# Turning the rows of 36 steps by DMA, over two 16-bit planes, in place of TensorE; and a first weight block loaded in quarters

## The chip, the cores and the metric

The kernel runs on one core of a Trainium2 chip. The metric is the time of one execution on the device in microseconds (us), less being better. The time before is 2451.24 us, the median of three runs (2449.57 to 2452.58).

## The reference

Input x has 128 sequences of 64 steps with 512 values each. Two layers are added to it in turn. Cut to what matters:

```python
# layer 0: a GRU over the 64 steps, then a linear layer with ternary weights
hs = gru(cond, x, W_ih, W_hh, b_ih, b_hh)           # 64 steps, one after another
x = x + einsum('bsi,oi->bso', hs, ternary(weight)) + bias
# layer 1: a causal convolution over the steps, then a mixture of experts
c = depthwise_causal_conv(x, cond) + b               # [128, 64, 512]
scores = softmax(c @ gate_w.T)                       # 64 experts, the best 6 per row
routed = sum over chosen experts of score * (silu(r @ w_gate) * (r @ w_up)) @ w_down   # at most 64 rows each
shared = silu(c @ sw_gate) * (c @ sw_up) @ sw_down   # 512 -> 704 -> 512, for all 8192 rows
x = x + routed + shared
```

## The kernel before

The work goes through one core in stages. First come the 64 steps of the GRU (loop over t, up to about 1220 us of the span), with the weights split into planes of fewer bits. Then comes the convolution (`conv_group`, to about 1280 us), as products with small Toeplitz matrices; it leaves its result c in SBUF, in two tiles `hids` of 32 steps each. `hid(t)` is the slice of step t: 128 sequences on the partitions, 512 values of 4 bytes along the row.

From there on the kernel goes through the 64 steps in 16 groups of NB = 4 (`shared(i)`, i from 0 to 15). Each group computes the shared expert with Winograd's seven products in place of eight (`winograd`, called by `Block.product` for up and gate and by `Down.product` for the way back). A product is two f32 matmuls of 256 columns; `PIECES` (44) is about the number of pieces that one `shared(i)` yields. Products add up in few PSUM buffers (`psx`, `psw`, `psz`, `y`), and VectorE and ScalarE take them out in between: `u2` (L853), `u3` (L858), `g1` (L864), `g2` (L867), `two` (L870). TensorE can't start the next sum in a buffer before that.

A product needs the values along the partitions, so the rows of each step are turned first. That is what `turn(t)` does, with four TensorE transposes of 128x128 into PSUM (L1128), and `route` copies them back over `hid(t)` on VectorE (L1138). From step TH = 32 on the turned rows also go to `xts` in HBM (L1144), for the second half of the groups. `route(its)` then computes the router's `lg` products (L1152), the softmax and the six best experts, for the groups `its`; `tab<-sc` stores the scores (L1196). `routing()` calls it for groups 2i+1 and 2i+2 while `shared(i)` runs (i from 0 to 7), and the main loop takes one step of it at every 44/20 of a piece. The memory of a group that is done is free for others: `sums_space(i)` uses the rows of group i-2 for the sums of the Winograd products, and `add_shared(i)` adds a group's result to the output with a DMA from GpSimd's queue (L1106).

What runs when is set by a planner: the instructions are recorded in the order of the program, and it then puts them in order on each engine by expected times and by priorities (`tc.issue_after` binds some). Each engine, and each engine's queue of DMA issues, then keeps to that order.

At the start the kernel loads the first step's input `xp` and the weights of the input gates, `raw_i[0]`, `raw_i[2]`, `raw_i[1]`, in halves of 512 KB (`load_halves`), all on SP's queue. TensorE's first products (`psy`) need `xp` and `raw_i[0]`, and VectorE and ScalarE split the weights into planes (`convert`).

Of the kernel before, what the change touches and what calls it, by code (L numbers as in the profile page):

```python
# [9 lines left out]
BF16 = mybir.dt.bfloat16  # L10
I32 = mybir.dt.int32
U8 = mybir.dt.uint8
F32R = mybir.dt.float32r
AF = mybir.ActivationFunctionType
ALU = mybir.AluOpType
# [4 lines left out]
P = 128  # L20
B = 128
T = 64
D = 512
KD = D // P
# [23 lines left out]
def adaln_ffn_kernel(  # L48
# [22 lines left out]
    nc = tc.nc  # L71
# [10 lines left out]
    xts = dram.tile([T // 2, P, D], F32, name="xts")  # L82
# [10 lines left out]
        out=before,  # L93
        in_=before,
# [11 lines left out]
    def load_rows(dst, src):  # L106

        return nc.sync.dma_start(out=dst, in_=src.rearrange("(k p) n -> p k n", p=P))
# [98 lines left out]
    HK = KD // 2  # L207
    HD = D // 2
    gis_ = ExitStack()
    ps_gi = gis_.enter_context(tc.tile_pool(name="ps_gi", bufs=1, space=PSUM))  # L210
    with (
# [19 lines left out]
        def planes(pool, name):  # L231
            return [pool.tile([P, KD, D], F32R, name=f"{name}{n}") for n in "hls"]

# [7 lines left out]
        raw_i = [st.tile([P, KD, D], F32, name=f"rawi{c}") for c in range(3)]  # L241
# [9 lines left out]
        cols = [slice(c * D, (c + 1) * D) for c in range(3)]  # L251
        xps, xns, parts_of = {}, {}, {}

        def load_xt(t, queue=nc.gpsimd):
            xps[t] = xpp.tile([P, KD, B], F32, name="xp")
            queue.dma_start(out=xps[t], in_=xT[t])
# [34 lines left out]
        def repeated(dst, row):  # L291
            nc.sync.dma_start(out=dst, in_=row.partition_broadcast(P))

        def load_halves(dst, src):
            for k in range(2):
                load_rows(dst[:, k * HK : (k + 1) * HK], src[k * HD : (k + 1) * HD])

        h = el0.tile([P, D], F32, name="h")
        bh = {0: io0.tile([P, D], F32, name="xn"), 1: el0.tile([P, D], F32, name="n")}

        load_xt(0, nc.sync)
        load_halves(raw_i[0], w_ih[:, cols[0]])
        load_halves(raw_i[2], w_ih[:, cols[2]])
        nc.sync.dma_start(out=h, in_=cond)
        load_xt(1, nc.sync)
        load_halves(raw_i[1], w_ih[:, cols[1]])
        load_rows(raw_h[0], w_hh[:, cols[0]])
        repeated(br, b_ih[cols[0]])
        repeated(bh[0], b_hh[cols[0]])
# [20 lines left out]
        def banks(c):  # L330
            pool = ps_gh if c == 1 else ps_gi
            return [pool.tile([P, D], F32, name=n) for n in BANKS[c]]
# [37 lines left out]
        def split_x(t):  # L370

            xp = xps.pop(t)
            cut = xpp.tile([P, KD, B], F32, name="xcut", bufs=1)
            parts_of[t] = [el0.tile([P, KD, B], F32R, name=f"x{n}") for n in "hls"]
            xh, xl, xs = parts_of[t]
# [46 lines left out]
        def place(t, n):  # L422

            if t < T - TAIL:
                return xpp.tile([P, KD, B], F32R, name=f"h{n}", bufs=1)
            return el0.tile([P, KD, B], F32R, name=f"x{n}")

# [63 lines left out]
        def cell_n(t, ps, r):  # L491
            a, b = ps
            n = el0.tile([P, D], F32, name="n")
            if a is None:
                nc.vector.tensor_add(n, b, bhn)
            else:
                nc.vector.scalar_tensor_tensor(n, a, WHOLE, bhn, ALU.mult, ALU.add)
                nc.vector.tensor_add(n, b, n)
            nc.vector.tensor_mul(n, n, r)
            nc.vector.tensor_add(n, n, gis.pop((t, 2)))  # L500
            nc.scalar.activation(n, n, AF.Tanh)  # L501
            nc.vector.tensor_sub(h, h, n)
            return n
# [15 lines left out]
        for c in (0, 2, 1):  # L519
            a, b = banks(c)  # L520
# [15 lines left out]
        n = cell_n(0, (None, first[2][1]), r)  # L536
# [41 lines left out]
        for t in range(1, T):  # L578
# [18 lines left out]
            n = cell_n(t, ps_n, r)  # L597
# [11 lines left out]
            if t in (1, 2):  # L609
# [9 lines left out]
                else:  # L619
                    sgn = wh0.enter_context(  # L620
                        tc.tile_pool(name="sgn", bufs=1, reuse_waits="tile")
                    ).tile([P, KD, D], F32R, name="sgn")
                    wf = wi.tile([P, KD, D], F32, name="q")
# [37 lines left out]
    TH = T // 2  # L661


    cum = ctx.enter_context(tc.tile_pool(name="cum", bufs=1)).tile([P, T, NE], U8, name="cum")
    first = ExitStack()
# [9 lines left out]
    def hid(t):  # L675
        return hids[t // TH][:, t % TH, :]
# [21 lines left out]
    with tc.tile_pool(name="ps_c", bufs=4, space=PSUM) as ps_c:  # L698
        for sl in range(NSL):
# [6 lines left out]
            for g in range(DS // 4):  # L706
# [4 lines left out]
                d = slice(g * 4, g * 4 + 4)  # L711
# [9 lines left out]
            if sl >= TAIL_AT:  # L721
# [3 lines left out]
                d = slice(0 if sl == TAIL_AT else 2 * DS * sl, 2 * DS * (sl + 1))  # L725
# [3 lines left out]
            for n in range(2):  # L729
                if sl == NSL - 2 + n:  # L730
                    d = slice(2 * DS * sl, 2 * DS * (sl + 1))
# [61 lines left out]
    NB = 4  # L793
# [3 lines left out]
    def behind(instructions, when=True):  # L797
        return tc.issue_after(instructions[-1].ins) if when and instructions else nullcontext()
# [303 lines left out]
    PIECES = 7 * full + 9  # L1102

    def add_shared(i):
        for t in range(i * NB, i * NB + NB):
            nc.gpsimd.dma_start(out=out_t[t], in_=rows_of(i)[:, t % NB], accum_op=ALU.add)  # L1106


    with (
# [10 lines left out]
        def turn(t):  # L1120

            if t in (2, 3):
                ps = ps_y.tile([P, D], F32, name="y")
            else:
                ps = ps_t1.tile([P, D], F32, name="pst1")
            ps = ps.rearrange("p (k b) -> p k b", k=KD)
            for k in range(KD):
                last = nc.tensor.transpose(ps[:, k, :], hid(t)[:, k * P : (k + 1) * P], ident)  # L1128
            return ps, last

        def route(its, turned={}):


            for i in its:
                for t in range(i * NB, i * NB + NB):
                    ps = turned[t] if t in turned else turn(t)[0]
                    with behind(marks, t in turned):
                        copied = nc.vector.tensor_copy(  # L1138
                            hid(t).rearrange("p (k b) -> p k b", k=KD), ps
                        )  # L1140
                    if t == NB - 1:
                        marks.append(copied)
                    if t >= TH:
                        nc.sync.dma_start(out=xts[t - TH], in_=hid(t))  # L1144
                    yield
# [21 lines left out]
            for n, i in enumerate(its):  # L1167
# [27 lines left out]
                for a in range(2):  # L1195
                    nc.sync.dma_start(  # L1196
                        out=tab_t[i * NB + 2 * a : i * NB + 2 * a + 2, :, D:].rearrange(
                            "t b e -> b t e"
                        ),
                        in_=sc[:, a::2, :NE],  # L1200
# [7 lines left out]
                for j in range(NB):  # L1208
                    t, r = i * NB + j, 2 * (j % 2) + j // 2
# [17 lines left out]
        def put_rows(i):  # L1227
            if i < NI:

                with tc.issue_after(loaded.ins):  # L1230
                    for t in range(i * NB, i * NB + NB):
                        (nc.gpsimd if i == 1 else nc.sync).dma_start(
                            out=tab_t[t, :, :D], in_=hid(t)
                        )
# [5 lines left out]
        for j in range(2):  # L1240
            nc.sync.dma_start(out=swdr[j * rest : (j + 1) * rest, :], in_=sw_down[full * P :, :])

        ahead = route([0])
        for _ in range(NB):
            next(ahead)
# [8 lines left out]
        for i in range(NI // 2):  # L1254
            put_rows(2 * i + 3)
            put_rows(2 * i + 4)

            def routing():
                if i == 0:
                    yield from ahead  # L1260
                its = [r for r in (2 * i + 1, 2 * i + 2) if r < NI]
                yield from route(its, second if i == 0 else {})

            routing_ = routing()
            done = 0
            for n, _ in enumerate(shared(i)):
                if done * PIECES <= n * 20:
                    with behind(products or marks, i == 0):
                        next(routing_, None)
                    done += 1  # L1270
            for _ in routing_:
                pass
            add_shared(i)
# [325 lines left out]
    for i in range(NI // 2 + 1, NI):  # L1599
        n = i - NI // 2 - 1  # L1600
        sums = None
        if i == NI - 1:
# [3 lines left out]
                out=sums, in_=out_t[i * NB : (i + 1) * NB].rearrange("t b d -> b t d")  # L1606
# [58 lines left out]
```

## Time and profile before

| | before |
|---|---|
| median of 3 runs | 2451.24 us (2449.57 to 2452.58) |
| profiled execution, its own time | 2452.42 us |
| its span | 2450.7 us |
| granted TensorE clock, mean | 0.999 |
| instructions | 32124 |
| TensorE transposes `pst<-ident,hid` and `y<-ident,hid` (L1128) | 256 |
| VectorE copies back (L1138) | 64, of 0.69 us |

The profile is one execution, so its times are compared with its own time and not with the median. PE is TensorE, PEld its weight loads (which overlap PE), DVE VectorE, ACT ScalarE, POOL GpSimd, SP the engine that issues most DMAs. In a line of a group, "out<-in" are the program's names, then come shapes and count, the busy time in us and the mean of one in ns, then the idle time before these instructions and what ended it. A line of the timeline has start, duration, engine, line, operation and count; one of the chain has start, duration and what. In a line of windows the numbers after an engine are busy us and, in brackets, instructions.

### The profile page before, as it was taken

How to read it: one execution, taken by the hardware profiler on the slowest of the kernel's cores; microseconds unless marked ns; L12 is line 12 of the kernel's file. 1: busy time of each engine (PE TensorE's matmuls, PEld its weight loads, DVE VectorE, ACT ScalarE, POOL GpSimd, SP SyncE). 2: the span in 40 equal slices, each digit the busy share in tenths (PEclk: the TensorE clock that was granted, in tenths of full speed). 3: DMA queues.
4: the chain of work that ended last, by engine and by line, in shares of the span. 5: the costliest groups of instructions: out<-in, count | busy, mean ns of one | idle time of the engine just before them, and what ended most of it. 6: DMA issues, size and time to landing. Idle time of an engine off the chain costs nothing.

```text
span 2450.7 us, 32124 instructions
## 1 busy us (share of the span) xinstructions
PE 2436.9 (99%) x12317; PEld 1883.7 (77%) x12317; DVE 1546.5 (63%) x3073; ACT 463.1 (19%) x847; POOL 445.8 (18%) x468
## 2 busy tenths in 40 slices
PE   9999999999999999999999999999999999999999
PEld 5888888888888888888896688888876666666667
DVE  8877777777777776777686566666653433343344
ACT  5211111111111111111122222222211111111111
POOL 1122221122112112211220000000012222222220
PEclk9999999999999999999999999999999999999999
DMA  5244443333232223222497112222468999899962
GB/s 183 68 95 81 82 80 63 61 69 65 56 61 56 56 56 62 56 52 52 142 343 270 24 23 44 62 59 61 116 174 287 300 290 312 267 330 293 283 175 52
DMA packets 464456, 322.33 MB, mean 132 GB/s; under 512 B 316592, under 2 KB 384176, under 8 KB 462128
## 3 DMA queue, kind: packets, MB, share of 16 engines
q1 hardware_dynamic: 435408, 246.34, 35.6%
q0 software_dynamic: 28896, 73.95, 13.5%
q8 instruction: 97, 1.59, 0.3%
q14 instruction: 55, 0.45, 0.1%
HBM read 233.44 MB, written 92.03 MB: 133 GB/s over the span
## 4 chain that ended last, share of the span: by engine, by line
PE 98%; DMA 1%; DVE 0%; issue 0%; ACT 0%; SPq 0%; POOL 0%; DVEq 0%; ACTq 0%
PE psa L336 9%; PE psx L336 9%; PE psw L336 9%; PE psx L824 8%; PE psw L824 8%; PE psz L824 8%; PE psy L336 5%; PE psb L336 5%; PE psz L336 5%; PE psf L336 5%; PE y L824 4%; PE py L1550 3%; PE pg L1524 3%; PE pu L1524 3%; PE y L1001 2%; PE psc L193 2%
## 5 line engine op out<-in xcount | busy, mean ns | idle before, releaser
L1534 DVE SCALAR_TENSOR_TENSOR a<-a,rw,pu 128x352 f32<-128x352 f32 x32 | 18.6, 580 | 213.4 <-PE pu L1524 213.4
L354 DVE SCALAR_TENSOR_TENSOR xs<-xl,xcut 128x512 fp32r<-128x512 f32 x63 | 103.6, 1644 | 66.0 <-POOL xl L353 66.0
L347 DVE TENSOR_SCALAR hcut<-pst 128x512 int32<-128x512 int32 x63 | 43.5, 691 | 129.8 <-PE pst L419 127.6
L1106 POOL DMA_DIRECT2D out_dram<-hid x32 | 27.7, 1006 | 449.6 <-issue 333.5
L353 POOL TENSOR_TENSOR xl<-xp,xcut 128x512 fp32r<-128x512 f32 x60 | 82.8, 1380 | 145.2 <-PE psa L336 145.1
L488 ACT ACTIVATE rz<-rz 128x512 f32<-128x512 f32 x64 | 40.5, 633 | 336.1 <-DVE rz L487 336.1
L433 ACT CAST hh<-hcut 128x512 fp32r<-128x512 f32 x61 | 37.9, 622 | 325.0 <-DVE hcut L347 325.0
L271 POOL DMA_DIRECT2D q<-in_x_dram x36 | 19.3, 537 | 409.7 <-DMA out_dram<-q 313.4
L1550 PE MATMUL py<-wd,aeT 128*64 128x512 f32 (+1 forms) x384 | 88.8, 597 | 0.0
L1524 PE MATMUL pg<-wg,xeT 128*64 128x352 f32 x512 | 81.2, 459 | 0.0
L1524 PE MATMUL pu<-wu,xeT 128*64 128x352 f32 x512 | 81.2, 459 | 0.0
L1561 POOL DMA_INDIRECT out_dram<-ys,idxp x32 | 47.0, 1469 | 183.4 <-DMA out_dram<-ys,idxo 103.7
L1561 POOL DMA_INDIRECT out_dram<-ys,idxo x32 | 45.0, 1407 | 174.3 <-DMA out_dram<-ys,idxp 168.1
L336 PE MATMUL psa<-wih1h,xh 128*128 128x512 f32 x252 | 74.5, 416 | 0.0
L271 POOL DMA_DIRECT2D xn<-in_x_dram x28 | 15.0, 536 | 319.1 <-DMA out_dram<-xn 258.3
L1524 PEld LDWEIGHTS pg<-wg,xeT 128*64 128x64 f32 x512 | 36.3, 136 | 47.4 <-issue 47.4
L864 ACT ACTIVATE g<-psx 128x256 f32<-128x256 f32 x80 | 30.7, 384 | 217.5 <-DVE aT L871 158.5
L501 ACT ACTIVATE n<-n 128x512 f32<-128x512 f32 x64 | 40.5, 633 | 163.3 <-DVE n L500 160.9
L336 PE MATMUL psw<-wih2h,xh 128*128 128x512 f32 x252 | 68.7, 394 | 0.0
L336 PE MATMUL psw<-wih2l,xl 128*128 128x512 f32 x252 | 68.5, 392 | 0.0
L336 PE MATMUL psa<-wih1l,xl 128*128 128x512 f32 x252 | 68.2, 392 | 0.0
L336 PE MATMUL psb<-wih1s,xs 128*128 128x512 f32 x252 | 68.1, 392 | 0.0
(429 smaller groups left out, 6170.2 us busy)
## 6 DMA issues: line engine op xcount, KB each, us to landing
wg<-in_w_gate_dram SPq DMA_DIRECT2D x64, 704.0 KB, 12.5
wu<-in_w_up_dram SPq DMA_DIRECT2D x64, 704.0 KB, 12.8
wd<-in_w_down_dram SPq DMA_DIRECT2D x64, 512.0 KB, 10.5
xc<-x1c SPq DMA_DIRECT2D x32, 512.0 KB, 6.8
xp<-in_xT_dram POOLq DMA_DIRECT2D x62, 256.0 KB, 2.9
tab<-hid SPq DMA_DIRECT2D x56, 256.0 KB, 4.3
wd<-in_w_down_dram SPq DMA_DIRECT2D x64, 192.0 KB, 10.7
q<-in_x_dram POOLq DMA_DIRECT2D x36, 256.0 KB, 2.9
```

Source lines behind the costliest of these rows:

```text
L193: i = nc.tensor.matmul(ps[rows, j].rearrange("p h (u t) -> p h u t", u=2), xcs[sl % NCB][:, rows, g * 4 + j], tzs[sl % NCB][:, :, :, g * 4 ...
L336: i = nc.tensor.matmul(ps, lhs[:, k, :], rhs[:, k, :], start=start and k == 0, stop=stop and k == KD - 1, skip_group_check=True,)
L347: return nc.vector.tensor_scalar(dst.bitcast(I32), src.bitcast(I32), LOW, None, ALU.bitwise_and)
L353: i = engine.tensor_sub(lo, full, cut)
L354: nc.vector.scalar_tensor_tensor(mix, lo.bitcast(F32), -SPLIT, cut, ALU.mult, ALU.add)
L488: nc.scalar.activation(r, r, AF.Sigmoid)
L501: nc.scalar.activation(n, n, AF.Tanh)
L824: i = nc.tensor.matmul(ps.rearrange("p (j b) -> p j b", b=P) if len(r.shape) == 3 else ps, lhs(k), r, start=(first and k == 0), stop=(k == ...
L1001: nc.tensor.matmul(gu.rearrange("p (j b) -> p j b", b=P), swr[:, k].rearrange("p w n -> p (w n)"), rows[:, k], start=(k == 0), stop=(k == ...
L1524: nc.tensor.matmul(acc[halves[j]], self.xeT[:, k, halves[j]], self.ws[j][which][:, k, :], start=(k == 0), stop=(k == KD - 1),)
L1550: nc.tensor.matmul(py[halves[j]], self.aeT[:n, c, halves[j]], self.ws[j][2][:n, c, :], start=(c == 0), stop=(c == len(ech) - 1),)
L1561: nc.gpsimd.indirect_dma_start(out=out, out_offset=bass.IndirectOffsetOnAxis(ap=(idxp[:CAP] if j == 0 else idxo)[:, q : q + 1], axis=0), i ...
```

## The change

From group 7 on (steps 28 to 63) the rows are turned by DMA. The DMA transpose moves 16-bit elements, so ScalarE first copies the lower halves of a step's 512 words into one plane of 512 16-bit values and the upper halves into another (L1152 of the changed kernel); both planes lie side by side in a flat buffer. One DMA transpose on SP's queue turns both planes into a second buffer (L1154). VectorE copies the two turned planes back, as lower and upper halves of the words of `hid(t)` (L1162). The buffers are slots of `hids` that are done with: steps 0 and 1 for the flat planes, 2, 3 and 7 for the turned ones. `pipelined` runs over the steps of the call, with the copies back LAG = 2 steps behind the copies out. From i = FREE = 3 on, the main loop takes a step of the routing at every 44/32 of a piece.

At the start, `raw_i[0]` is loaded in four quarters of 256 KB in place of two halves, and `xp` of step 0 by ScalarE's queue in place of SP's.

```diff
-        def load_halves(dst, src):
-            for k in range(2):
-                load_rows(dst[:, k * HK : (k + 1) * HK], src[k * HD : (k + 1) * HD])
+        def load_parts(dst, src, n=2):
+            for k in range(n):
+                load_rows(
+                    dst[:, k * KD // n : (k + 1) * KD // n], src[k * D // n : (k + 1) * D // n]
+                )
...
-        load_xt(0, nc.sync)
-        load_halves(raw_i[0], w_ih[:, cols[0]])
-        load_halves(raw_i[2], w_ih[:, cols[2]])
+        load_xt(0, nc.scalar)
+        load_parts(raw_i[0], w_ih[:, cols[0]], KD)
+        load_parts(raw_i[2], w_ih[:, cols[2]])
...
-        load_halves(raw_i[1], w_ih[:, cols[1]])
+        load_parts(raw_i[1], w_ih[:, cols[1]])
...
+        FREE = 3
+        LAG = 2
+        flat_at, turned_at = (0, 1), (2, 3, 2 * NB - 1)
+
+        def plane(t, n):
+            return hid(t).bitcast(U16)[:, n * D : (n + 1) * D]
+
+        def word_halves(t):
+            return hid(t).bitcast(U16).rearrange("p (d h) -> p d h", h=2)
+
+        def pipelined(steps):
+            for n in range(len(steps) + LAG):
+                for w in range(2):
+                    if n < len(steps):
+                        at = flat_at[n % len(flat_at)]
+                        nc.scalar.copy(plane(at, w), word_halves(steps[n])[:, :, w])
+                        if w:
+                            nc.sync.dma_start_transpose(
+                                out=hid(turned_at[n % len(turned_at)])
+                                .bitcast(U16)
+                                .rearrange("p (m b) -> p m b", b=P),
+                                in_=hid(at).bitcast(U16),
+                            )
+                    if n >= LAG:
+                        t, at = steps[n - LAG], turned_at[(n - LAG) % len(turned_at)]
+                        nc.vector.tensor_copy(word_halves(t)[:, :, w], plane(at, w))
+                        if w and t >= TH:
+                            nc.sync.dma_start(out=xts[t - TH], in_=hid(t))
+                    yield
+
         def route(its, turned={}):
-            for i in its:
+            apart = its[0] > 2 * FREE
+            if apart:
+                yield from pipelined([t for i in its for t in range(i * NB, i * NB + NB)])
+            for i in its if not apart else ():
                 for t in range(i * NB, i * NB + NB):
...
-                if done * PIECES <= n * 20:
+                if done * PIECES <= n * (20 if i < FREE else 32):
```

More of the change, by code (lines that the diff above doesn't have):

```diff
@@ L12 @@
 U8 = mybir.dt.uint8
+U16 = mybir.dt.uint16
 F32R = mybir.dt.float32r
```

## The prediction

> **What bounds the kernel now.** I read the page first: its busy shares, then the chain of waits that ended last.
>
> ```profile
> PE 2436.9 (99%) x12317; PEld 1883.7 (77%) x12317; DVE 1546.5 (63%) x3073; ACT 463.1 (19%) x847; POOL 445.8 (18%) x468
> PE 98%; DMA 1%; DVE 0%; issue 0%; ACT 0%; SPq 0%; POOL 0%; DVEq 0%; ACTq 0%
> ```
>
> TensorE is never free, so work taken off it is worth its full time, until another engine makes it wait. An average doesn't settle that, so I read the stages that the change touches: the table by windows, with one pass of `shared` from 1467.5 to 1527.
>
> ```profile
> core 0: us, PE busy (x) PEld busy (x) DVE busy (x) ACT busy (x) POOL busy (x), PEclk, DMA share, GB/s
> 1470.00:1530.00 60.00, 60.00 (x306) 48.63 (x305) 37.76 (x114) 14.37 (x28) 3.74 (x5) 1.00 0.21 41
> 1467.50:1490.00 22.50, 22.50 (x114) 18.22 (x112) 14.41 (x30) 3.33 (x9) 1.73 (x2) 1.00 0.28 59
> 1522.80:1567.00 44.20, 44.20 (x232) 35.49 (x231) 26.37 (x72) 11.09 (x22) 1.73 (x2) 1.00 0.26 68
> 1572.30:1582.50 10.20, 10.20 (x51) 8.48 (x50) 6.14 (x22) 0.74 (x2) 1.73 (x2) 1.00 0.28 33
> ```
>
> PE has no gap here at full clock; VectorE is busy for 63%, ScalarE for 24%. Next, the timeline of PE, for what a turned step costs, and the groups by shape for the copies.
>
> ```profile
> 1473.19 1.03 PE L824 MATMUL psw<-hid,sw1first 128*128 128x256 f32 x4
> 1474.05 0.60 PE L1128 MATMUL pst<-ident,hid 128*128 128x128 f32 x4
> 1474.49 1.03 PE L824 MATMUL psx<-hid,sw0first 128*128 128x256 f32 x4
> ...
> L1138 DVE COPY hid<-pst 128x512 f32<-128x512 f32 x62 | 42.8, 691 | 16.7 <-PE pst L1128 16.3
> L347 DVE TENSOR_SCALAR xcut<-xp 128x512 int32<-128x512 int32 x63 | 29.6, 471 | 5.6 <-DVE xs L354 0.4
> L377 ACT CAST xh<-xcut 128x512 fp32r<-128x512 f32 x63 | 38.8, 616 | 36.0 <-PE psa L336 35.7
> ```
>
> The 0.60 us overlaps its neighbours; from the start of the four transposes to the next product is 0.44 us. Last, the DMA issues (KB each, us from issue to landing) and the start of the chain.
>
> ```profile
> x1c<-q SPq DMA_DIRECT2D x36, 256.0 KB, 4.5
> xts<-hid SPq DMA_DIRECT2D x32, 256.0 KB, 2.0
> ...
> 1.26 3.99 DMA rawi<-in_w_ih_dram
> 5.38 6.11 PE psy L336 x8
> ```
>
> **What is removed.** Steps 28 to 63 are 36 steps with 144 transposes (256 stand in the order of TensorE's instructions before, 112 in that of the changed program as built). At 0.435 us for four, the mean of the neighbouring groups, 36 x 0.435 = 15.7 us leaves a PE that has no gap. A check from the chain: the passes start 59.50 us apart, but the one that routes only four steps takes 56.01. Of these 3.49 us, 1.72 are 16 fewer `lg` products (3.60 against 1.88) and about 0.2 two fewer `lgT` transposes; 1.55 us for four steps is 0.39 each, or 14.0 for 36. I take 15.7 and keep 14.0 as an end. The 36 copies out of PSUM on VectorE (0.691 us) go too.
>
> **What is added.** For each step there are two ScalarE copies of 128x512 halves, one DMA transpose of 256 KB on SP's queue, and two VectorE copies back. ScalarE: 72 x about 0.62 (the row of L377) = 45 us over some 130 us that are now 24% busy; hidden. VectorE: the trace has no 16-bit copy from SBUF to SBUF. The nearest row is L347's 0.471 us, one SBUF source of the same width; the upper end is 0.69, that of nearly every other 128x512 row. I take 0.47, so 0.94 a step in place of 0.69.
>
> **Where waits can come from.** Engines run in order, so a late transpose holds VectorE's copy, and behind it the additions that empty PSUM for the next products; that is how a DMA reaches PE. On ScalarE, the copy of step n+2 reuses the flat buffer of step n and waits for its transpose to land; behind it wait `u2` and `g1` (0.37 us each), which PE needs too. One round of two steps is therefore landing time L + two ScalarE copies (1.23) + two handovers (about 0.17 together, an idle time that VectorE shows at a product's end): s = (L + 1.4) / 2 per step.
>
> What time has a step? In the order as built, the planner has drawn the transposes forward, into gaps that it expected. Placing each pair of copies by the VectorE instruction ahead of it and that one's time in this trace gives 3 steps before 1467; 8 steps from 1467.5 to 1490; 20 from 1522.8 to 1567; 5 from 1572.3 to 1582.5. Without their own transposes (8 steps each in the first two stretches, 3.5 us) these allow (22.5 - 3.5) / 8 = 2.38, (44.2 - 3.5) / 20 = 2.04 and 10.2 / 5 = 2.04 us per step. The stall is 8 x (s - 2.38) + 25 x (s - 2.04), where positive.
>
> L isn't in the trace. The nearest row is `xts<-hid`: as many bytes, same queue, same stage, SBUF rows read: 2.0 us. Above it stands `x1c<-q`, as many bytes written in small pieces (64 B): 4.5. A transpose reads whole rows and writes small pieces, but into SBUF; I take 2.8, nearer to the low end, since what is quick there (the reading side, the queue, the size) is shared. Then s = 2.1. Some transposes stand behind an `xts` store on SP's queue, whose issue takes about 0.4 us; s = 2.2 on the whole. Stall: 25 x 0.16 = 4 us. At L = 2.0 it is nothing; at 4.5 s is 2.95 and the stall 4.6 + 22.8 = 27 us.
>
> [...] The rows have 109 ns for a 128x128 transpose on TensorE, in f32 (0.435 / 4), and nothing for one by DMA. [...]
>
> **The start.** The first product waits for 512 KB of `rawi`, issued at 1.26 behind `xp` and landed at 5.25. Now a quarter goes first at about 0.81, with `xp` from ScalarE's queue beside it. Landing takes between 2.9 us (a quiet 256 KB `xp`) and the 4.0 of the half: 3.7 to 4.8, so 0.5 to 1.5 earlier. VectorE's conversions, the bound of the first 40 us (10.0 of 10 busy from 30 to 40), start earlier by as much. I take 1.0. One more issue on SP (0.5 us) puts off the loads behind it, which are not waited for until 10.9.
>
> **The sum.** The profiled execution took 2452.42 us, with a span of 2450.7. 2452.4 - 15.7 - 1.0 + 4.0 = 2439.7; it lies 1.2 above the median of the runs, so 2438.5.
>
> **Rivals.** A, the forecast: the transposes keep up nearly; chance 0.55.
>
> B, slower: the transpose's landing takes the place of TensorE as the bound of the three stretches. It decides from a stall of 16.7 us: 33 s = 16.7 + 19.0 + 51, s = 2.63, L = 3.8. At L = 4.5 the stall of 27 less 16.7 gives +10.6, or 2461.8. For it: small pieces were slow in `x1c` (4.5), and the `add_shared` transfers share the engines; against it: DMA is only 26% busy there. Chance 0.28.
>
> C, VectorE becomes the bound: the stretch of 44.2 us holds 26.4 - 5.5 + 40 x 0.47 = 39.7 us of its work in 40.7, so it fits only just. At 0.69 a copy it is 48.5, 7.8 too many, and with about 1 and 2.8 in the other two stretches 11.5 us of the gain is lost: 2451.2 - 16.7 + 11.5 = 2446. Chance 0.10.
>
> D, stalls and gains cancel, with L about 3.6 to 4.1: no change, 2451; 0.07.
>
> **How the numbers follow.** About 0.2%, or 4.9 us, is what a measurement of this kernel can tell from no change. A and most of C make it faster: 0.63; D and the edge of C give 0.09 for the same; B 0.28. The range goes from full gain with no stall and 1.5 at the start (2451.2 - 17.2 = 2434) to B at L = 4.5 (2462).
>
> **What would show it.** Right: no L1131 transposes of pst after the first 28 steps; passes from 1467 on of about 56 us plus stalls; PE idle or late behind VectorE's L1162, which waits for DMA by some 0.1 us a step; landings of 2.5 to 3.1 us; the first psy before 4.9. Wrong: landings above 3.8, with ScalarE's L1152 waiting for DMA and PE idle by 0.5 us or more a step; or L1162 at 0.6 us or more, with VectorE busy throughout from 1520 to 1565.

## The result, and the profile after

The changed kernel takes 2469.38 us, the median of four runs (2467.63 to 2473.44), against 2451.66 for the kernel before (four runs, 2449.57 to 2452.58). The ratio is 1.0076, with a 95% interval from 1.0058 to 1.0093: slower by about 18 us. The forecast of 2438.5 and the upper end of its range, 2462, were both missed. The profiled execution took 2468.16 us, with a span of 2466.5 us and a mean granted clock of 0.994.

First the page of the changed kernel, its busy times and the shares of its chain.

```profile
PE 2431.4 (99%) x12173; PEld 1872.6 (76%) x12173; DVE 1545.9 (63%) x3109; ACT 502.8 (20%) x919; POOL 448.7 (18%) x468
PE 92%; DMA 4%; DVE 2%; ACT 1%; issue 0%; SPq 0%; POOL 0%; DVEq 0%; ACTq 0%; POOLq 0%
```

There are 144 fewer TensorE instructions, as told, but their time fell by 5.5 us only, and 8% of the chain now lies outside TensorE. The table by windows says where and why.

```profile
core 0: us, PE busy (x) PEld busy (x) DVE busy (x) ACT busy (x) POOL busy (x), PEclk, DMA share, GB/s
1470.00:1480.00 10.00, 5.15 (x15) 3.38 (x13) 3.44 (x9) 4.22 (x8) 0.85 (x1) 0.69 0.94 155
1480.00:1490.00 10.00, 8.81 (x27) 7.25 (x28) 5.78 (x16) 4.33 (x10) 0.00 (x0) 0.63 0.64 171
...
1540.00:1550.00 10.00, 4.53 (x11) 2.97 (x12) 3.88 (x10) 5.66 (x10) 0.00 (x0) 0.66 0.90 179
1610.00:1620.00 10.00, 7.30 (x25) 5.88 (x26) 5.19 (x13) 1.54 (x4) 1.73 (x2) 0.83 0.69 146
```

Two things go wrong in the same places. TensorE is idle for up to 5.5 of the 10 us of a window, and the clock column falls to between 0.63 and 0.83, which it did nowhere in these stages before. A busy TensorE hides the second: 8.81 of 10 us look well used, but 27 instructions were done there, where a full window at a clock of 1.00 holds about 50 (51 in the 10.2 us from 1572.3 of the kernel before). The timeline of PE shows both at once.

```profile
1470.34 1.03 PE L827 MATMUL y<-hid,st 128*128 128x256 f32 x4
1474.82 2.07 PE L827 MATMUL psw<-hid,sw1first 128*128 128x256 f32 x4 [3.46 <-DVE hid L1026]
...
1481.19 2.07 PE L827 MATMUL psw<-hid,st 128*128 128x256 f32 x4 [2.59 <-DVE u L861]
...
1545.05 2.07 PE L827 MATMUL psw<-hid,sw1first 128*128 128x256 f32 x4 [5.80 <-DVE hid L1026]
```

A product of four such matmuls takes 1.03 us before the gap of 3.46 us and 2.07 after it. VectorE's L1026 and L861 ended the gaps, but they had themselves stood behind the turning copies, as the view of who waits for the transposes (L1154) and the chain between 1534 and 1546 tell.

```profile
L1154 SPq DMA_TRANSPOSE hid<-hid x36: 1232/1279/2667, 1449.5 to 1608.2; - x36
  ACT hid L1152: 56.7, 25
  DVE hid L1162: 44.2, 22
DMA to landing us min/median/max: 3.0/3.2/8.8
```

```profile
1536.20 7.74 DMA hid<-hid
...
1543.97 0.46 DVE hid L1162
...
1544.49 0.61 ACT hid L1152
```

A transpose keeps SP's queue for 1.23 us at least and lands after a median of 3.2 us; one of them took 7.74, and a VectorE copy, then a ScalarE copy into the flat buffer that it had held, came straight after.

**The balance.** I lined up the starts of the same products in both traces. The changed kernel is ahead by 2.8 us at 1408 (the start), behind by 6.8 at the group that starts at 1527.0 in the trace before, by 18.4 at the one of 1586.5, by 20.8 at 1646.0 and by 16.1 from 1819.5 to the end. From 1408 on that is a loss of 18.9 us in place of a gain of 15.7, so stalls took 34.6 us. TensorE's idle gaps make up 20.8 us of them, and products that ran longer than the median of their own group inside the three stretches of halved clock another 8.2 (4.7 from 1474 to 1487, 2.0 from 1538 to 1550, 1.5 from 1612 to 1617). The remaining 5.6 are not located: they are spread in small steps.

The idle time is in few places. The steady run of steps from 1545 to 1581 issued a transpose every 2.4 us or so, landed them in 3.1 to 4.0 us, and has 3.6 us of gaps in it and just behind it. The other large gaps, 3.46, 2.59, 5.80 and 2.92, make up 14.8 us, and stand behind transposes that landed late. Three of the four follow transposes beside an `add_shared`: the one issued at 1468.2, between adds issued at 1468.0 and 1471.0, landed in 5.08 us, those at 1536.2 and 1539.5, beside adds at 1535.5 and 1536.0, in 7.74 and 5.83, and those at 1598.2 and 1600.5, beside adds at 1597.2 and 1597.8, in 8.77 and 7.03. The gap of 2.59 follows the pair issued at 1474.3 and 1475.6, which landed in 4.67 and 4.16 us; there the profile has a load of instructions, a packet of 16 KB on the queue q8 at 1476.9. Being issued close together isn't enough to be late: the pair at 1586.3 and 1587.7, with neither beside it, landed in 3.19 and 3.08. The adds in the stretch from 1465 to 1605 landed later too, in 4.1 to 9.1 us with a median of 5.4 (L1109), against 4.0 to 6.1 and 4.9 before (L1106).

### The profile page after: what moved, and what is told of

Its sections match the earlier page's. It is cut to its first block, busy times and chain, and to the rows that moved or that the text cites. A ratio compares the mean times of both kernels' runs of the same rounds, so it can differ in the third digit from the quotient of the medians.

```text
span 2466.5 us, 32042 instructions
## 1 busy us (share of the span) xinstructions
PE 2431.4 (99%) x12173; PEld 1872.6 (76%) x12173; DVE 1545.9 (63%) x3109; ACT 502.8 (20%) x919; POOL 448.7 (18%) x468
## 4 chain that ended last, share of the span: by engine, by line
PE 92%; DMA 4%; DVE 2%; ACT 1%; issue 0%; SPq 0%; POOL 0%; DVEq 0%; ACTq 0%; POOLq 0%
PE psw L339 9%; PE psa L339 9%; PE psx L339 9%; PE psw L827 7%; PE psx L827 7%; PE psz L827 7%; PE psb L339 5%; PE psy L339 5%; PE psf L339 5%; PE psz L339 5%; PE y L827 4%; PE py L1588 3%; PE pg L1562 3%; PE pu L1562 3%; DMA hid<-hid 3%; PE y L1004 2%
## 5 line engine op out<-in xcount | busy, mean ns | idle before, releaser
L1109 POOL DMA_DIRECT2D out_dram<-hid x32 | 27.7, 1003 | 469.1 <-issue 277.1
L858 DVE TENSOR_TENSOR u<-u,y 128x256 f32<-128x256 f32 x80 | 33.6, 420 | 70.2 <-PE y L827 67.7
L339 PE MATMUL psy<-wih0s,xs 128*128 128x512 f32 x252 | 68.2, 392 | 1.0 <-DVE rz L487 1.0
```

Source lines behind the costliest of these rows:

```text
L339: i = nc.tensor.matmul(ps, lhs[:, k, :], rhs[:, k, :], start=start and k == 0, stop=stop and k == KD - 1, skip_group_check=True,)
```

## The experiments

Four explanations stood against each other. **The order**: nothing ties a copy to its piece of the loop, and the planner drew the 36 steps forward, in numbers of about 11, 20 and 5 per pass where the loop gives 8, so that transposes come close together and reach into the ends of passes. **The adds**: `add_shared` slows the transposes that it meets. **The transpose itself**: it is too slow at any order, as rival B said. **The clock**: idle gaps are paid again by products at half clock. Every ratio below is against runs of the kernel before on the same chip, with its 95% interval.

### The start alone

The first two hunks of the diff, on the kernel before.

> Only the start of the change (quarters of the first weight block, first input by ScalarE's queue), rows turned by TensorE as before. The comparison of the two traces has the GRU ahead by 2.9 us from 121 us on, so theory W (the loss comes from waiting for transposes) expects 2.9 us less than before, ratio 0.9988. The prediction's own term was 1.0 us, ratio 0.9996. If the start is what made it slower, the ratio is above 1.

It took 2449.74 us, ratio 0.9992 (0.9983 to 1.0001); in its trace the work is ahead by 2.8 to 2.95 us from 121 us to the end. The first product starts only 0.6 us earlier, and the first 40 us add to that. A part of it is the clock: from 40 to 50 us its mean is 0.66 in the kernel before and 0.83 here, since it is halved near 40 us for 6.8 us before and for 3.4 here. This stretch varies with the kernel. Versions below with the same start are ahead by 1.7 us where they have 6.8 us of it, by 2.2 to 3.2 where they have 3.4, and by 3.2 and 4.2 where they have none; and the one-hop kernel of the last experiment, which starts like the kernel before but has 3.4 us of it, is ahead by 1.6. So with a stretch of the same length the start edit is worth some 0.5 to 1.7 us, and the rest of the lead isn't shown to be its own.

### Without the adds

```diff
-            add_shared(i)      # in the loop over i from 0 to 7
```

This kernel leaves out what the adds would have written.

> The changed kernel without the DMAs that add the shared expert's rows of groups 0 to 7 to the output (32 transfers of 256 KB from GpSimd's queue; that part of the output is left out). Theory W1 (a transpose lands in 3.1 us, and late ones, 5 to 9 us, are those beside these transfers): no landing over 4.0 us, PE idle under 6 us from 1440 to 1720, no halved clock there, 2436 to 2445 us. Rival W2 (late ones wait for each other and for stores on SP's queue): landings up to 8 us stay, time within 5 us of 2469. Rival V (the copies on VectorE and ScalarE cost the time, not the waits): 2469.

It took 2453.7 us, ratio 1.0006 (0.9997 to 1.0016): 15.7 us less than the changed kernel, but still no gain, and the expectation of one was missed. PE's gaps fell from 20.8 to 13.4 us and the halved clock in these stages from 24 to 3.4. ScalarE still waits for transposes for 42.5 us (56.7 before this edit) and VectorE for 30.1 (44.2). The gap of 3.75 us at 1473.7 is there without any add near it: a pair issued at 1470.5 and 1471.9 released its waiter only at 1475.25, 4.7 us after the first issue. A load of instructions falls into it, its 16 KB packet at 1473.0; the table of DMA queues from 1472.5 to 1474.9 has it beside the transposes' packets, and a DMA share (tenths in 40 slices) near nothing from 1473.9 on:

```profile
DMA  9999999893479999999999990000001100001000
q8 instruction: 1, 0.02, 3.3%
```

Lined up as above, this kernel is ahead by 2.25 us at 1408 and behind by 2.3 at the end, where 15.7 were to be gained: 20 us of stalls, against 34.6 with the adds. So the adds cost some 14 us of the stalls, but they aren't the whole of it.

### The copies bound to their pieces

ScalarE's copies are put behind the last ScalarE instruction of their own piece, VectorE's behind the last VectorE one, so that the planner can't draw them forward.

```diff
-                nc.scalar.copy(self.u2, ps)
+                acts.append(nc.scalar.copy(self.u2, ps))
...                                        # the other acts and adds alike
-                        nc.scalar.copy(plane(at, w), word_halves(steps[n])[:, :, w])
+                        with behind(acts):
+                            nc.scalar.copy(plane(at, w), word_halves(steps[n])[:, :, w])
...
-                        nc.vector.tensor_copy(word_halves(t)[:, :, w], plane(at, w))
+                        with behind(adds):
+                            nc.vector.tensor_copy(word_halves(t)[:, :, w], plane(at, w))
```

> The changed kernel with the copies out and back bound behind the ScalarE and VectorE instructions of their own piece, so that eight steps are turned in each pass, one per 2.4 us, and none is drawn forward. Theory W1: the transposes away from the add transfers land in 3.1 us and keep up with 2.4 us a step; the first two of each pass still land in 5 to 8 us and stop PE for 2 to 4 us each pass (5 passes), some with a halved clock behind: 2442 to 2458 us. W2: with one or two in flight all land in 3.1 to 3.6, 2434 to 2438. V: same work, 2469.

It took 2439.37 us, ratio 0.9949 (0.9934 to 0.9964), about 30 us less than the changed kernel with the same arithmetic, transposes and adds, and between the two ranges that were expected. The steps stand 8 to a pass, the PE gaps are 3.4 us in all, and the clock is never halved in these stages. The first two of the windows above:

```profile
1470.00:1480.00 10.00, 10.00 (x48) 8.81 (x47) 7.11 (x19) 5.60 (x13) 0.00 (x0) 1.00 0.54 97
1480.00:1490.00 10.00, 10.00 (x48) 8.79 (x48) 7.71 (x21) 5.14 (x12) 0.00 (x0) 1.00 0.81 171
```

48 instructions in each window stand against 15 and 27. The five passes with turned steps gain 3.0, 2.9, 2.6, 1.3 and 0 us; full gain would be 15.7, and 9.6 arrive. Bound, the steps also keep clear of most adds: the adds ahead of the first two of these passes are issued by 1465.8 and 1522.3, the steps of these passes from 1469.7 and 1526.2 on. The waits that are left:

```profile
ACT hid L1155 <- DMA hid<-hid: 20.3, 19, 2.0
DVE hid L1166 <- DMA hid<-hid: 14.2, 21, 2.4
```

### Bound, and the adds held back

On top of that, the adds of group i-1 are issued at piece 30 of the next pass in place of the end of their own.

```diff
+                if i and n == DEFER:      # DEFER = 30
+                    add_shared_late(i - 1)
...
-            add_shared(i)
```

> As x4_bound, and the add transfers of a group are held back until piece 30 of the next pass, when the transposes are done (they follow a one-column copy on GpSimd that reads a result of that piece). Theory W1: all landings 3.0 to 3.7 us, PE idle under 5 us from 1440 to 1720, no halved clock: before - 2.9 - 15.7 + some 2 = 2433 to 2439 us. W2: as x4_bound. V: 2469.

It took 2446.42 us, ratio 0.9975 (0.9965 to 0.9985), worse than with the binding alone and than the 2433 to 2439 expected. The passes with turned steps gain 3.0, 2.8, 2.6, 0.85 and 1.4 us, the same sum as without this edit within a microsecond. So once the steps are spread, and begin when most adds are over, holding the adds back brings these passes nothing more that can be told. The loss is one new wait that the edit made, in the pass of group 1, where no row is turned by DMA: the late add still reads rows that the next sums are to overwrite. The timeline of PE there:

```profile
1381.04 1.03 PE L828 MATMUL psx<-hid,sw 128*128 128x256 f32 x4
1385.38 2.07 PE L828 MATMUL psw<-hid,sw 128*128 128x256 f32 x4 [3.32 <-DVE g L872]
```

A gap of 3.32 us was followed by 6.8 us at half clock, and that pass lost 6.1 us: almost twice the gap.

### Bound, at a slower pace; and the pace alone

The loop takes a step of the routing at every 44/28 of a piece in place of 44/32, once with the binding and once without.

```diff
-                if done * PIECES <= n * (20 if i < FREE else 32):
+                if done * PIECES <= n * (20 if i < FREE else 28):
```

> x4_bound with a routing step at every 44/28 of a piece in place of 44/32: a step is turned per 2.7 us and not 2.4. Theory W1: s = (3.1 + 1.4) / 2 = 2.25 leaves more room, fewer short waits, 2435 to 2438 us. Theory V: no change against x4_bound, 2439.

> The changed kernel with the routing's pace of y9_pace28 (44/28 of a piece), but without binding the copies to their pieces, so that the planner may draw them forward as in the change. If the planner's order is the cause (theory W1), the pace in the program means nothing: 36 steps in three thick stretches as in the change, 2455 to 2475 us. If the pace alone is what was too quick, it is as y9_pace28: 2433 to 2438.

With the binding it took 2434.7 us, ratio 0.9928 (0.9915 to 0.9942), the fastest version here and faster than both kernels. Without it, 2465.35 us, ratio 1.0054 (1.0037 to 1.0071). First the fast one's transposes and who waits for them:

```profile
L1157 SPq DMA_TRANSPOSE hid<-hid x36: 1231/1236/2392, 1471.7 to 1704.4; - x36
  ACT hid L1155: 13.3, 13
  DVE hid L1166: 5.2, 11
DMA to landing us min/median/max: 3.0/3.1/4.0
```

No landing is over 4.0 us, TensorE has no gap over 0.4 us and no halved clock in the turning stages, and the passes gain 3.54, 3.54, 3.55, 3.54 and 1.99 us. Their sum is 16.2, of which some 0.4 us make up for a loss in the pass ahead of them: this kernel is ahead by 1.73 us at the first `lg` and by 17.39 in the last stage, so 15.7 come from the turned rows. That is the whole forecast term. Without the binding the timeline of PE has the old picture:

```profile
1545.86 2.08 PE L827 MATMUL psx<-hid,sw0first 128*128 128x256 f32 x4 [7.13 <-ACT u L856]
```

The order is what decides: the same pace costs 13 us or brings 17. The pace then settles the rest, from 9.6 to 15.7.

### A longer lag, free and bound

LAG = 3 and one flat buffer and one turned buffer more, which need FREE = 4, so that 28 steps are turned by DMA and not 36 (the expectations below count 32).

```diff
-        FREE = 3
-        LAG = 2
-        flat_at, turned_at = (0, 1), (2, 3, 2 * NB - 1)
+        FREE = 4
+        LAG = 3
+        flat_at, turned_at = (0, 1, 4), (2, 3, 5, 6)
```

> The changed kernel, its order left to the planner as in the change, with the ring of y1_bound_lag3 (lag three, 32 steps). Theory W1 with the planner's order as the cause: a longer ring lets the planner draw the transposes still closer together, and they still run beside the add transfers: 2450 to 2470 us. Rival L (the lag of two alone is too short): as y1_bound_lag3, 2434 to 2440.

> x4_bound with the copies back three steps behind in place of two, three flat and four turned buffers (0, 1, 4 and 2, 3, 5, 6), which are free from group 9 on only: 32 steps by DMA, saving 13.9 us. x4_bound loses about 6 of its 15.7 us to short waits: ScalarE waits 20 us and VectorE 14 us for landings. If the ring of two is what is short (theory W1), these waits nearly go: 2434 to 2437.5 us, under x4_bound's 2439.4. If the rest is lost elsewhere (VectorE's and ScalarE's work, theory V), four steps less by DMA make it 2440 to 2442.

Unbound it took 2457.64 us, ratio 1.0021 (1.0011 to 1.003). With more buffers, and eight steps fewer by DMA, it takes 12 us less than the changed kernel, but there are still PE gaps of 2.24, 4.38, 1.17 and 2.31 us, and 10.2 us of halved clock. Bound it took 2440.06 us, ratio 0.9947 (0.9934 to 0.9961). There the transposes cost nothing that PE shows: no gap over 0.4 us in the turning stages, and 12.2 us of PE's time gone with 112 transposes. But a pass gains 2.77 us in place of 3.49; taken from start to start, the products of `psz` take about 1.8 us more in all, in an order that the planner drew differently, and no run tests that. The time lies in the range that was expected if VectorE's and ScalarE's work were the cause, but PE never waits for it, and 28 steps can bring 12.2 us and not 13.9. Bound, the longer lag hid a landing of 5.18 us; unbound, it didn't stop the bunches (the gap of 4.38 us).

This trace also shows what a load of instructions goes with. Each of its four passes issues three transposes 1.3 to 1.4 us apart. In three passes they all land in 3.1 to 3.4 us. In the fourth a load's packet of 16 KB stands at 1710.1, and the three issued from 1705.6 to 1708.3 land in 3.20, 5.18 and 4.62. The three of the fourth, with the load in the table of DMA queues from 1709.5 to 1713:

```profile
DMA to landing us min/median/max: 3.2/4.6/5.2
q8 instruction: 1, 0.02, 1.9%
```

Five traces have landings one by one: the changed kernel, this one, the unbound one with the longer lag, the fastest, and the next below. All of their 22 landings over 4.0 us ran beside packets of the adds (11, some of them beside a load too) or of a load of instructions (11), while nine whole steps issued within 1.6 us of the one ahead, with neither beside them, took 3.1 to 3.6 us. The loads stand in every version, the kernel before too, where one of 16 KB comes about every 25 us; no run takes them away, so their part is read from the traces alone.

### One transpose for each plane

On the bound version, each plane is turned as soon as it is there, so 72 transposes of 128 KB in place of 36 of 256.

```diff
-                        if w:
-                            nc.sync.dma_start_transpose(out=hid(...)..., in_=hid(at).bitcast(U16))
+                        nc.sync.dma_start_transpose(out=plane(..., w)..., in_=plane(at, w))
```

> x4_bound with each plane turned by a DMA of its own (72 transposes of 128 KB in place of 36 of 256 KB), issued as soon as its copy out is done. If landing is mostly a fixed time, 2.6 to 3.0 us each, the engines' share is doubled and the time is that of x4_bound or up to 4 us more. If it goes with the size (1.6 to 2.2 us), the waits shrink: 2434 to 2438 us.

It took 2450.69 us, ratio 0.9993 (0.9984 to 1.0002), 11 us more than with whole steps and more than either expectation.

```profile
L1156 SPq DMA_TRANSPOSE hid<-hid x72: 1188/1211/2359, 1449.0 to 1718.0; - x72
DMA to landing us min/median/max: 2.4/2.4/4.3
```

Half the bytes take 2.4 us to land in place of 3.05, and SP's time for an issue hardly changes (1.21 against 1.24), so a step occupies SP's queue for 2.4 us. PE's gaps grew from 3.4 to 11 us in all.

### A gap by itself

To measure the clock's part without any transpose by DMA, in the kernel before one small TensorE transpose in the pass of group 4 waits for a chain of small DMAs on SP's queue, of one hop or of three, and the later products of the pass stand behind it.

```diff
+                if i == 4 and n == 28:
+                    src = tokens[-1]
+                    for k in range(HOPS):          # 1 or 3
+                        far = sm.tile([P, 32], F32, name=f"far{k}")
+                        nc.sync.dma_start(out=far, in_=src)
+                        src = far
+                    ...
+                    with behind(products):
+                        forced.append(nc.tensor.transpose(ps[:32, :P], src, ident))
```

> The kernel before, in which TensorE is made to wait once, in the pass of group 4: behind a product it transposes 32 columns that one small DMA has just copied from a result of that pass. Nothing else is changed. Measures what idle time of TensorE costs beside itself. Theory G (a gap of about 3 us or more is followed by a halved clock, one under 2 us isn't): the gap is some 1 to 2 us, no halved clock follows, and the groups behind are later by the gap alone. Rival: any gap is followed by a halved clock.

> As z_wait1 with three small DMAs one behind the other, so a gap of some 5 to 6 us. Theory G: the granted clock falls to half during the gap and stays there for 3.4 to 7 us, and the groups behind are later by the gap and another 1.5 to 3.5 us. Rival (the clock is not what was lost in the changed kernel): later by the gap alone.

One hop took 2452.61 us, ratio 1.0005 (0.9995 to 1.0014): it left no gap over 0.2 us on PE, where one of 1 to 2 was expected, and the pass grew by 0.52 us, the price of the added work and its order. Three hops took 2457.16 us, ratio 1.0019 (1.001 to 1.0029). The timeline of PE, and the window around it:

```profile
1565.59 0.28 PE L1283 MATMUL pst<-ident,far 128*32 128x128 f32 x1 [2.32 <-DMA far<-far]
```

```profile
1565.00:1570.00 5.00, 4.41 (x15) 3.55 (x16) 1.79 (x5) 0.59 (x2) 0.00 (x0) 0.66 0.02 3
```

The gap is 2.32 us and the pass grew by 4.66; less the 0.52 of the one-hop kernel that is 4.14. The halved clock lasts 3.4 us, with half of it lost 1.7, and 2.32 + 1.7 = 4.0. The medians of the two kernels, of ten runs each, differ by 4.55 us. So the clock's part is shown by itself: this gap costs nearly twice its length.

## Why the prediction was wrong

**What is removed: right.** TensorE's time for transposes, from the start of each to the start of the next instruction, fell by 15.72 us in the changed kernel, and the bound version at the slower pace gained 15.7. The check of 14.0 was the worse of the two figures.

**The copies: right.** VectorE's take 0.452 us (0.47 taken) and ScalarE's 0.617. Rival C fell: VectorE didn't become the bound.

**The start: more than taken, in part by luck.** The first product came 0.41 us earlier, and the work after it 2.9, where 1.0 was taken. The term left out the halved stretch near 40 us, which was 3.4 us long in this trace and 6.8 in the one before, and which isn't shown to follow from the edit; with stretches of the same length 1.0 lies among what the traces show.

**The stall term: the step that failed.** It was sized at 4 us and measured 34.6. The formula of a round fits roughly: with L = 5.08 it gives s = 3.2, and the pairs from 1466.9 to 1488.1 stand 3.0 to 3.9 us per step apart; with L of 3.3 it gives 2.35, and the steady run shows about 2.4. That run even has 3.6 us of gaps, as much as the whole term. Two of its inputs were wrong. One is L as a single number: it is 3.05 us alone, near the 2.8 taken, 4.2 and 4.7 for the pair that met a load of instructions, and 5.0 to 8.8 for the six that ran longest beside adds. The prediction saw the planner draw the steps forward, and took from that only how much time a step has, not that its transposes would then meet the adds, with no room left for a late one; the adds it weighed under rival B alone, against a DMA share of 26%. It also put no price on a transpose's own issue, 1.23 us on SP's queue, which spaces a pair. The other is the price of an idle microsecond, taken as one microsecond. The runs of the last experiment show 4.1 for 2.3, and in the changed kernel the halved clock cost 8.2 us on top of 20.8.

**Rival B** had the right sign and lay 7.6 us short, with a landing above 3.8 us as its mechanism. The mean of the 32 landings that the trace has is 3.9 us, so its bound was passed, but by eight landings of 4.2 to 8.8; the median is 3.2, and bound versions with the same transpose gain. So the transpose was not too slow: it was badly placed. Of what was to show the forecast wrong, ScalarE's L1152 waiting for DMA and PE's gaps of 0.5 us or more a step (20.8 for 36 steps) came true, and landings above 3.8 us in nine of the 32.

**Beside the nearest row.** The transpose's eight blocks of 128x128 landed together in 3.05 us. The plain `xts<-hid` of as many bytes, a store to HBM, took 2.0 in the trace before, so it was too quick a stand-in.

## What to carry to other kernels

Where a planner may move a new DMA and the copies around it, its landing time alone (3.05 us here, up to 8.8 beside adds) doesn't price it: look in the order as built at what else moves then, and at how much time the buffers leave for one that lands late. Bind such work to the pieces of the loop that it was written into, and let the loop issue it more slowly than a round of its buffers takes: a step per 2.7 us brought the full gain here, where a round allows one per (3.05 + 1.4) / 2 = 2.2. Where TensorE is otherwise never idle, allow for a gap that costs more than its length: in these runs gaps of 2.32 and 3.32 us cost 4.1 and 6.1, while that of 5.80 was followed by only 2.0 more.

## What the runs showed of the hardware

In the passes of `shared` the clock was halved in stretches of 3.4 us or multiples of it (3.4, 6.8, 10.2, 13.7). There gaps of up to 1.81 us were never followed by one; 2.25 and 2.31 were not, 2.28 and 2.32 were, for 3.4 us; 2.92 and 3.75 had 3.4, 3.24, 3.32, 5.80 and 7.13 had 6.8, 4.38 had 10.2, and 3.46 with 2.59 soon after had 13.7, but 3.73 with 4.61, in the unbound version at the slower pace, had 6.8. So in these runs the edge is near 2.3 us, and a gap's length alone doesn't tell how long the halved stretch is.

The issue of a DMA transpose took SP 1.21 us for 128 KB and 1.24 for 256, and its landing 2.4 and 3.05 us. All of them moved 16-bit elements, and no run has another width. The two that were issued at 1474.3 and 1475.6 in the changed kernel show as 2112 packets with 0.52 MB, some 250 B each.

A transpose that lands in 3.0 to 4.0 us without them took up to 8.8 beside accumulating DMAs from GpSimd's queue, and up to 5.8 beside a load of instructions of 16 KB.
